# Softmax rows of the first layer turned by block transposes and an exchange through HBM, in a two-layer attention and recurrence kernel

## The chip, the cores and the metric

The kernel runs on one core of a Trainium2 chip. The time is device microseconds of one execution. The core has a matrix engine (TensorE, PE in the profile), a vector engine (VectorE, DVE), an activation engine (ScalarE, ACT), a general engine (GpSimd, POOL) and SyncE (SP), which here only issues DMA transfers. Everything is float32. A float32 matmul stands in the profile as two records, a transpose as one.

## The reference

32 batches, each an x of 128x512 and a context of 128x512, go through two layers.

```python
def layer0(x_c, x_s):                       # (128 channels, 512 positions)
    Mn = Wn @ inorm(x_c) + bn;  Mm = Wm @ inorm(x_s) + bm
    A  = softmax(Mn.T @ Mm, axis=-1)        # 512 x 512, rows t, columns s
    Ml = Wl @ x_s + bl
    Mo = Ml @ A.T                           # sum over s of Ml[c, s] A[t, s]
    return Wo @ Mo + bo + x_c
```

The second layer reads the result as 128 time steps of 512 features. It has a layer norm, a shift by one step, five mixed inputs with low-rank corrections, projections to r, k, v, g and a decay w, a recurrence over time in 32 heads of 16 (state = k v + w state; out = r (u k v + state)), a norm per head, an output projection added to the input, and a feed-forward part with squared relu and a sigmoid gate.

What matters here is the product with A.T. The scores come with t on partitions and s along the free axis, and softmax is taken along the free axis. The product sums over s, so TensorE wants A with s on partitions: the softmax rows must be turned.

## The kernel before

The 32 batches go in 8 groups of 4. `layer0(b)` (line 806) does one batch of the first layer. `layer1(g, xs)` (line 1135) does the second layer for a group, its four batches side by side as 512 columns; the batches of the next group are called inside it through `ahead`, so that both layers' instructions can be mixed.

Nothing is issued in the order in which it is written. Every call on `K` is only recorded as an operation with a cost (`cost`, line 291) and its dependences; `schedule` (line 325) then lays the operations out on the five engines by list scheduling. An operation's rank is its index, lowered by the length of the chain behind it and moved by `SHIFTS` (line 63): a number for each stage, and with a "+" one more for the last groups. A stage is a part of the work: "first0" to "first3" are the four layer-0 batches of a group, "front", "mixes", "gates", "recurrence", "values", "levels", "outputs", "head", "norm", "squares" and "rows" are parts of layer 1. The order that results is written out by hand to the engines' queues. `pace` (line 375) then looks at the loads: a load of over 500 ns is put behind a matmul of the plan, away from stretches where PE has very many small instructions. SP carries out its queue in order, so a paced load holds what stands behind it on SP until that matmul is done.

Tensors live in pools of slots that the planner hands out: 8 PSUM banks, 44 work tiles of 128x512 (`t`), 40 small ones of 128x64 (`small`), 2 `rk`, 3 `wide` of 128x1024, 4 rings of a 512x512 weight (`wring`).

In `layer0`, for each block tb of 128 positions t, one matmul gives the scores (128x512) in a bank; DVE takes the row maximum and corrects it; ACT takes the exponent into a work tile and sums it into `den`; DVE takes the reciprocal and scales the tile (line 863). The four tiles are kept in `e`. Then (lines 866 to 876), for each block sb of 128 positions s, PE transposes four 128x128 blocks into one bank, ACT copies the bank to a work tile `at`, and PE multiplies `vals` (Ml folded with Wo, s on partitions) with it, adding up over sb into the bank `po`. DVE adds the bias and x.

The constants of the first layer are loaded and folded at the start (lines 650 to 689) in tiles of their own: `WnT`, `WmT`, `Wl0`, `WoT0`, `nat0`, `nat1`, `bn_bc`.

All instructions recorded through `K` carry line 246 in the profile.

Of the kernel before, what the change touches and what calls it, by code (L numbers as in the profile page):

```python
# [12 lines left out]
F32 = mybir.dt.float32  # L13
AF = mybir.ActivationFunctionType
ALU = mybir.AluOpType
# [3 lines left out]
P = 128  # L19
# [3 lines left out]
S = 16  # L23
G = 4
NG = B // G
N = G * L
NC = E // P
# [2 lines left out]
DM, NMIX, DD = 32, 5, 64  # L30
C = 64
LEVELS = (4, 8, 16, 32)
T_SLOTS, SMALL_SLOTS, W_SLOTS, WIDE_SLOTS = 44, 40, 4, 3
Q4 = 4
EPS = 1e-5


# [23 lines left out]
SWITCH = 95  # L61
ROUNDS, TRACE, BLAME = 16, 20000, 0.001
SHIFTS = {
    "first0": -289, "first0+": -139, "first1+": -80, "first2": -32, "first2+": 88,
    "first3": -12, "first3+": 216, "front": 28, "front+": 197, "gates": -508, "gates+": 16,
    "head": -270, "head+": 164, "levels0": -88, "levels0+": -263, "levels2": -188,
    "levels2+": -623, "mixes": 64, "mixes+": -66, "norm": 56, "norm+": -145,
    "outputs0": -369, "outputs0+": -26, "outputs2": -287, "outputs2+": -673,
    "recurrence0": -21, "recurrence0+": -92, "recurrence2": 12, "recurrence2+": -88,
    "rows": 76, "rows+": 170, "squares": -98, "squares+": 56, "values0": -35,  # L70
    "values0+": -187, "values2": 33, "values2+": 116,
}
REACH, PULL = 200, 0.003
WORDS, REFILL = 280, 3200
# [19 lines left out]
class View:  # L94
# [5 lines left out]
    def at(self, slot):  # L100
        ap = self.tensor.on(slot)
        for name, args, kw in self.chain:
            if name == "view":
                offset, dims = args
                ap = bass.AP(ap.tensor, ap.offset + offset, [list(ap.ap[0]), *[list(d) for d in dims]])
            else:
                ap = getattr(ap, name)(*args, **kw)
        return ap
# [15 lines left out]

    def to_broadcast(self, shape):
        return self._then("to_broadcast", shape)

    def view(self, offset, *dims):
        return self._then("view", offset, dims)
# [245 lines left out]
def pace(order):  # L375


    tensor = [op for op in order if op.engine == "PE"]
    ends = [op.end for op in tensor]
    dense = [(op.start, op.end) for op in tensor if op.words >= 64]  # L380
    begins = [s for s, _ in dense]

    def clear(a, b):
        i = bisect.bisect_left(begins, b) - 1
        return i < 0 or dense[i][1] <= a

    behind, at = {}, 0.0
    for op in order:
        if op.calls[0][1] != "dma_start" or op.landing < 500 or not op.after:
            continue  # L390
        latest = min(a.start for a in op.after) - op.landing - 5000
        i = bisect.bisect_left(ends, max(op.start, at))
        while i < len(ends) and ends[i] <= latest and not clear(ends[i], ends[i] + 2500 + 2 * op.landing):
            i += 1
        if i < len(ends) and ends[i] <= latest:
            op.behind = tensor[i]
            behind.setdefault(tensor[i], []).append(op)
            at = ends[i] + op.landing
    paced, met = [], set()
    for op in order:  # L400
        met.add(op)
        if op.behind is None or op.behind in met:
            paced.append(op)
        paced += [x for x in behind.get(op, []) if x in met]
    return paced
# [203 lines left out]
def xattn_then_rwkv(ctx: ExitStack, tc: tile.TileContext, a: dict, out: bass.AP):  # L609
    nc = tc.nc  # L610

    const = ctx.enter_context(tc.tile_pool(name="const", bufs=1))
    psum = ctx.enter_context(tc.tile_pool(name="psum", bufs=1, space=PSUM))

    def slots(tag, count, shape, space=const):
        return [space.tile(shape, F32, tag=f"{tag}{i}", name=f"{tag}{i}") for i in range(count)]
# [1 line left out]
    banks = Pool(slots("bank", 8, [P, 512], psum))  # L618
    work = Pool(slots("t", T_SLOTS, [P, 512]))
    small = Pool(slots("small", SMALL_SLOTS, [P, 64]))  # L620
    rks = Pool(slots("rk", 2, [P, 4 * N]))
    wides = Pool(slots("wide", WIDE_SLOTS, [P, 2 * N]))
    weights = Pool(slots("wring", W_SLOTS, [P, NC * E]))
    ats = [Pool(slots(f"at{q}_", 1, [P, 2 * G * 2 * C])) for q in range(Q4)]
    vps = Pool(slots("vp", 1, [P, 2 * G * Q4 * 2 * DM]))
    for t in [t for p in ats for t in p.tiles] + vps.tiles:
        nc.vector.memset(t, 0.0)  # L627

    K = Program(nc, tc)
# [7 lines left out]
    def wide(shape=(P, 2 * N)):  # L637
        return View(Tensor(wides, list(shape)))

    def st_(*shape):  # L640
        return View(Tensor(small, [P, *shape]))


    ident = const.tile([P, P], F32, tag="ident", name="ident")
# [3 lines left out]
    eps = const.tile([P, 1], F32, tag="eps", name="eps")  # L648
    nc.gpsimd.memset(eps, EPS)
    w0 = {}  # L650
    for n in ("WnT", "WmT", "Wl0", "WoT0"):
        w0[n] = const.tile([P, P], F32, tag=n, name=n)
        nc.scalar.dma_start(w0[n], a[n])
    bias4 = const.tile([P, len(BIASES)], F32, tag="bias4", name="bias4")
    nc.scalar.dma_start(bias4, a["bias4"])
# [3 lines left out]

    nat = {}  # L660
    for i, n in enumerate(("WnT", "WmT")):
        nat[n] = const.tile([P, P], F32, tag=f"nat{i}", name=f"nat{i}")
        pn = banks.tiles[4 + i]
        nc.tensor.transpose(pn[:, 0:P], w0[n], ident)
        nc.vector.tensor_copy(nat[n], pn[:, 0:P])
# [2 lines left out]
    nc.tensor.matmul(pq[:, 0:P], nat["WnT"], nat["WmT"], start=True, stop=True)  # L668
    nc.vector.tensor_copy(wq, pq[:, 0:P])
    qwc = const.tile([P, 3], F32, tag="qwc", name="qwc")  # L670
    bn_bc = const.tile([P, P], F32, tag="bn_bc", name="bn_bc")
    nc.vector.tensor_copy(bn_bc, bias["bn"].to_broadcast([P, P]))
    pw = banks.tiles[2]
    for i, (left, right) in enumerate(
# [131 lines left out]
    def layer0(b):  # L806
        K.stage = ("first", b, str(b % G))
        x_c, x_s = wt(), wt()
        K.held = begun.get(b - 2)
        K.sync.dma_start(x_c, a["x"][b])  # L810
        K.held = begun.get(b - 2)
        K.sync.dma_start(x_s, a["ctx_2048"][b])
        stats = st_(2, 6)
        K.vector.bn_stats(stats[:, 0, :], x_c)
        K.vector.bn_stats(stats[:, 1, :], x_s)
        mv, rstd = mean_rstd(stats, 2)
        xn = []
        for i, src in enumerate((x_c, x_s)):
            xn.append(wt())
            K.vector.tensor_scalar(  # L820
                xn[i], src, mv[:, i, 0:1], rstd[:, i : i + 1], ALU.subtract, ALU.mult
            )
        x_n, y_n = xn
        pm = bank()
        K.tensor.matmul(pm, wq, x_n, start=True, stop=True)
        q = wt()
        K.scalar.activation(q, pm, AF.Identity, bias=qb)

        pc = bank()
        with K.bunch(480):  # L830
            for tb in range(NC):
                K.tensor.matmul(
                    pc[:, tb : tb + 1], x_n[:, tb * P : (tb + 1) * P], wb, start=True, stop=True
                )
        same = st_(NC)
        K.vector.tensor_scalar(same, pc[:, 0:NC], cb, None, ALU.add)


        pv = bank()
        for sb in range(NC):  # L840
            K.tensor.matmul(
                pv[:, sb * P : (sb + 1) * P], x_s[:, sb * P : (sb + 1) * P], wol,
                start=True, stop=True,
            )
        vals = wt()
        K.scalar.copy(vals, pv)


        e = []
        for tb in range(NC):  # L850
            sc = bank()
            if tb == 0:
                begun[b] = K.ops[-1]
            K.tensor.matmul(sc, q[:, tb * P : (tb + 1) * P], y_n, start=True, stop=True)
            nmax, den = st_(1), st_(1)
            K.vector.tensor_reduce(nmax, sc, AX.X, ALU.max, negate=True)

            part = same[:, tb : tb + 1]
            K.vector.scalar_tensor_tensor(nmax, nmax, part, part, ALU.subtract, ALU.add)
            t = wt()  # L860
            K.scalar.activation(t, sc, AF.Exp, bias=nmax, accum_out=den)
            K.vector.reciprocal(den, den)
            K.vector.tensor_scalar(t, t, den, None, ALU.mult)
            e.append(t)
        po = bank()
        for sb in range(NC):
            pt = bank()
            for tb in range(NC):
                K.tensor.transpose(
                    pt[:, tb * P : (tb + 1) * P], e[tb][:, sb * P : (sb + 1) * P], ident  # L870
                )
            at = wt()
            K.scalar.copy(at, pt)
            K.tensor.matmul(
                po, vals[:, sb * P : (sb + 1) * P], at, start=(sb == 0), stop=(sb == NC - 1)
            )
        K.vector.scalar_tensor_tensor(x_c, po, bol, x_c, ALU.add, ALU.add)
        return x_c


    def norm_shift(xs, w, bname, row, g):
        xns = []
# [53 lines left out]
    def recurrence(c, ex, xk, xr, xv, wk, wr, s0m):  # L936
# [13 lines left out]

        VP = G * Q4 * 2 * DM
        vp = View(Tensor(vps, [P, 2 * VP]))
        at = [View(Tensor(p, [P, 2 * G * 2, C])) for p in ats]
        for i in range(2):
            pt = bank()
            for b in range(G):
                K.tensor.transpose(pt[:, b * P : (b + 1) * P], v[i][:, b * P : (b + 1) * P], ident)
            K.scalar.copy(
                vp.view(i * VP, (2 * DM, G * Q4), (DM + S, 2), (1, S)),
                pt.rearrange("p (x y j) -> p x y j", x=G * Q4, y=2),  # L960
            )
# [56 lines left out]
        for l in LEVELS:  # L1018
# [4 lines left out]
            for x in range(2):  # L1023
# [4 lines left out]
                )  # L1028
            pa = [bank() for _ in range(Q4)]
            with K.bunch(1522):  # L1030
# [396 lines left out]
```

## Time and profile before

| what | value |
|---|---|
| runs | 1791.61, 1793.8, 1794.59 us; median 1793.8 |
| span of the profiled execution | 1791.5 us, 45991 instructions |
| granted TensorE clock, mean | 0.996 |
| DMA traffic | 87.27 MB, 14.5% of the 16 DMA engines' time on the SP queue |
| full 128x128 transposes on PE | 896 with 128 columns, 512 of them in layer 0 |

The profile counts busy time for each engine over the span, from the first to the last instruction. "128*128" behind a matmul is the part of the array that it uses, then the size of what goes through. A duration of a matmul is the time until its result is out; matmuls overlap, so the step from one start to the next is shorter. In a group of instructions the numbers behind the bar are busy time in us, mean ns of one, and the engine's idle time ahead of them with what ended it. In a table of windows, a number in brackets counts instructions, PEclk is the granted clock as a share of full speed, and the last two columns are the DMA engines' share and GB/s.

### The profile page before, as it was taken

How to read it: one execution, taken by the hardware profiler on the slowest of the kernel's cores; microseconds unless marked ns; L12 is line 12 of the kernel's file. 1: busy time of each engine (PE TensorE's matmuls, PEld its weight loads, DVE VectorE, ACT ScalarE, POOL GpSimd, SP SyncE). 2: the span in 40 equal slices, each digit the busy share in tenths (PEclk: the TensorE clock that was granted, in tenths of full speed). 3: DMA queues.
4: the chain of work that ended last, by engine and by line, in shares of the span. 5: the costliest groups of instructions: out<-in, count | busy, mean ns of one | idle time of the engine just before them, and what ended most of it. 6: DMA issues, size and time to landing. Idle time of an engine off the chain costs nothing.

```text
span 1791.5 us, 45991 instructions
## 1 busy us (share of the span) xinstructions
PE 1759.7 (98%) x20434; PEld 903.8 (50%) x20434; DVE 1195.1 (67%) x2466; ACT 681.9 (38%) x1198; POOL 313.4 (17%) x329
## 2 busy tenths in 40 slices
PE   7999999999999999999999999999999999899998
PEld 5535653456434564346543465435654445435543
DVE  8958884469835697357963679636884765866661
ACT  3424531355322553234522445224442334324321
POOL 2240015100051000500006000150010420320011
PEclk9999999999999999999999999999999999899999
DMA  6100131022020221102111021110211201000110
GB/s 192 36 0 3 43 113 66 6 64 79 30 71 1 70 74 49 52 2 88 61 48 47 2 87 61 53 41 2 88 61 59 74 25 49 3 24 3 50 36 35
DMA packets 61943, 87.27 MB, mean 49 GB/s; under 512 B 20336, under 2 KB 21488, under 8 KB 61744
## 3 DMA queue, kind: packets, MB, share of 16 engines
q1 hardware_dynamic: 61024, 84.06, 14.5%
q8 instruction: 160, 2.62, 0.6%
q14 instruction: 39, 0.32, 0.1%
q10 hardware_dynamic: 720, 0.26, 0.1%
HBM read 75.93 MB, written 8.39 MB: 47 GB/s over the span
## 4 chain that ended last, share of the span: by engine, by line
PE 89%; ACT 3%; DVE 3%; issue 3%; POOL 2%; DMA 0%; POOLq 0%; SPq 0%; ACTq 0%; DVEq 0%
PE bank L246 89%; POOL t L246 1%; DVE t L246 1%; ACT at L246 1%; DVE small L246 1%; ACT wide L246 1%; ACT t L246 0%; DMA t<-in_x_dram 0%; ACT L246 0%; DVE rk L246 0%; DVE at L627 0%; DVE vp L627 0%; POOLq L1423 0%; POOL small L246 0%; PE bank L677 0%
## 5 line engine op out<-in xcount | busy, mean ns | idle before, releaser
L246 PE MATMUL bank<-t,wring 128*128 128x512 f32 x1024 | 467.9, 599 | 0.8 <-POOL t L246 0.6
L246 PE MATMUL bank<-wring,t 128*128 128x512 f32 x768 | 340.4, 596 | 0.7 <-DVE t L246 0.7
L246 POOL TENSOR_TENSOR t<-t,t 128x512 f32<-128x512 f32 x192 | 239.2, 1282 | 426.9 <-DVE t L246 426.4
L246 PEld LDWEIGHTS bank<-t,wring 128*128 128x128 f32 x1024 | 187.2, 190 | 237.6 <-issue 211.9
L246 DVE TENSOR_TENSOR t<-bank,t 128x512 f32<-128x512 f32 (+1 forms) x256 | 143.8, 584 | 195.7 <-PE bank L246 114.8
L246 PE MATMUL bank<-t,t 128*128 128x512 f32 x512 | 255.8, 609 | 0.7 <-ACT t L246 0.2
L246 POOL TENSOR_TENSOR small<-small,neg_half 128x1 f32<-128x1 f32 (+1 forms) x96 | 65.4, 689 | 1046.0 <-DVE small L246 1046.0
L246 PEld LDWEIGHTS bank<-wring,t 128*128 128x128 f32 x768 | 143.3, 190 | 188.5 <-issue 177.6
L246 ACT COPY t<-bank 128x512 f32<-128x512 f32 (+1 forms) x240 | 132.7, 587 | 275.4 <-PE bank L246 250.3
L246 ACT ACTIVATE t<-bank 128x512 f32<-128x512 f32 x120 | 71.6, 597 | 376.4 <-PE bank L246 338.1
L246 DVE SCALAR_TENSOR_TENSOR t<-bank,vec,t 128x512 f32<-128x512 f32 x192 | 133.1, 743 | 99.3 <-PE bank L246 82.0
L246 PEld LDWEIGHTS bank<-ident,t 128*128 128x128 f32 x900 | 105.2, 141 | 71.0 <-issue 50.7
L246 ACT ACTIVATE wide<-rk,par 128x512 f32<-128x512 f32 x128 | 85.3, 714 | 131.7 <-DVE rk L246 130.9
L246 PE MATMUL bank<-ident,t 128*128 128x128 f32 x900 | 132.5, 277 | 0.3
L246 PEld LDWEIGHTS bank<-wide,rk 32*64 32x64 f32 x8192 | 95.5, 132 | 54.5 <-ACT wide L246 18.2
L246 PE MATMUL bank<-t,wv 128*128 128x512 f32 x256 | 122.6, 601 | 0.0
L246 PEld LDWEIGHTS bank<-t,t 128*128 128x128 f32 x512 | 86.0, 192 | 68.9 <-issue 40.3
L246 DVE COPY_PREDICATED at<-level,bank 128x512 f32<-128x512 int32 x192 | 120.1, 702 | 0.0
L246 PE MATMUL bank<-wide,rk 32*64 32x64 f32 x8192 | 105.5, 234 | 7.3 <-ACT wide L246 5.8
L246 ACT ACTIVATE t<-bank,small 128x512 f32<-128x512 f32 x128 | 87.5, 689 | 64.4 <-DVE small L246 63.8
L246 DVE TENSOR_REDUCE small<-bank 128x1 f32<-128x512 f32 x128 | 86.2, 683 | 24.0 <-PE bank L246 23.3
L246 DVE SCALAR_TENSOR_TENSOR t<-t,vec,t 128x512 f32<-128x512 f32 x128 | 92.0, 756 | 0.6
(114 smaller groups left out, 1828.1 us busy)
## 6 DMA issues: line engine op xcount, KB each, us to landing
t<-in_ctx_dram SPq DMA_DIRECT2D x32, 256.0 KB, 3.3
t<-in_x_dram SPq DMA_DIRECT2D x32, 256.0 KB, 3.7
wring<-in_WgT_dram SPq DMA_DIRECT2D x8, 1024.0 KB, 5.0
wring<-in_WkT_dram SPq DMA_DIRECT2D x8, 1024.0 KB, 5.1
wring<-in_WrT_dram SPq DMA_DIRECT2D x8, 1024.0 KB, 6.2
wring<-in_WoT_dram SPq DMA_DIRECT2D x8, 1024.0 KB, 5.2
out_dram<-t SPq DMA_DIRECT2D x32, 256.0 KB, 2.0
wring<-in_WfkT_dram SPq DMA_DIRECT2D x7, 1024.0 KB, 6.6
```

Source lines behind the costliest of these rows:

```text
L246: done[op] = f(*[real(x) for x in args], **{k: real(x) for k, x in kw.items()})
```

## The change

For the batches 4 to 31 (`blocks = b >= G`) the softmax rows are turned in another way; batches 0 to 3 keep the old one.

- The scaling by the reciprocal of `den` goes from DVE to ACT.
- DVE transposes each 128x512 tile in blocks of 32x32 (`vector.transpose`), reading with a stride of four elements and writing into half of a wide tile `turned`, 128x1024, that two tiles tb share. Within a block the turn is then done; which block lies on which group of 32 partitions is not.
- `exchange` puts that right: one DMA on SP's queue stores `turned` (512 KB) into a slot in HBM, a second one loads it back into another wide tile, with the 32-partition blocks in their places. Each batch has two such exchanges, one for each half of t.
- The product with `vals` runs over halves: for each half of t four matmuls of 256 columns, eight in all, in place of four of 512.
- The 16 PE transposes, the four banks for them and the four ACT copies of the batch go.
- A pool `turns` of six 512 KB slots in HBM is new. `pace` skips a DMA whose source is a tile of the planner, so the exchange's transfers aren't put behind a matmul.
- Pool sizes: work 44 to 42, wide 3 to 6, `small` 40 to 6 with 28 new `tiny` tiles of 128x16 beside it. The seven first-layer constants used only at the start lie in wide tiles now.
- `SHIFTS` has new numbers, among them "first1", "first1+", "first2+", "constants" and "front+".

```diff
-T_SLOTS, SMALL_SLOTS, W_SLOTS, WIDE_SLOTS = 44, 40, 4, 3
+T_SLOTS, SMALL_SLOTS, TINY_SLOTS, W_SLOTS, WIDE_SLOTS, RK_SLOTS, TURN_SLOTS = 42, 6, 28, 4, 6, 2, 6
 Q4 = 4
+QR = P // Q4
...
-    "first0": -289, "first0+": -139, "first1+": -80, "first2": -32, "first2+": 88,
-    "first3": -12, "first3+": 216, "front": 28, "front+": 197, "gates": -508, "gates+": 16,
...
+    "constants": -196, "constants+": 29, "first0": -289, "first0+": 238, "first1": 5,
+    "first1+": -319, "first2": -112, "first2+": 127, "first3": -12, "first3+": 210, "front": 23,
+    "front+": 310, "gates": -497, "gates+": 215, "head": -270, "head+": 201, "levels0": -58,
...
         if op.calls[0][1] != "dma_start" or op.landing < 500 or not op.after:
+            continue
+        if isinstance(op.calls[0][2][1], View):
             continue
...
+    dram = ctx.enter_context(tc.tile_pool(name="dram", bufs=1, space=bass.MemoryType.DRAM))
+    turns = Pool(slots("turn", TURN_SLOTS, [P, 2 * N], dram))
...
-        w0[n] = const.tile([P, P], F32, tag=n, name=n)
+        w0[n] = wides.tiles[i // 2][:, i % 2 * P : (i % 2 + 1) * P]
...
         e = []
+        blocks = b >= G
...
             K.vector.reciprocal(den, den)
-            K.vector.tensor_scalar(t, t, den, None, ALU.mult)
-            e.append(t)
+            if not blocks:
+                K.vector.tensor_scalar(t, t, den, None, ALU.mult)
+                e.append(t)
+                continue
+            K.scalar.activation(t, t, AF.Identity, scale=den)
+            if tb % 2 == 0:
+                turned = wide()
+            K.vector.transpose(
+                turned.view(tb % 2 * P, (QR, NC), (2 * P, Q4), (1, QR)),
+                t.view(0, (P, NC), (1, Q4), (Q4, QR)),
+            )
+            if tb % 2:
+                e.append(exchange(turned))
         po = bank()
-        for sb in range(NC):
+        for h in range(2 if blocks else 0):
+            for sb in range(NC):
+                K.tensor.matmul(
+                    po[:, h * 2 * P : (h + 1) * 2 * P], vals[:, sb * P : (sb + 1) * P],
+                    e[h].view(sb * QR, (P, 2), (2 * P, Q4), (1, QR)),
+                    start=(sb == 0 and h == 0), stop=(sb == NC - 1), skip_group_check=True,
+                )
+        for sb in range(0 if blocks else NC):
             pt = bank()
...
+    def exchange(of):
+        between, to = View(Tensor(turns, [P, 2 * N])), wide()
+        K.sync.dma_start(between, of)
+        K.sync.dma_start(
+            to.rearrange("p (i f) -> p i f", i=Q4),
+            between.whole(0, (2 * P, P), (QR * 2 * N, Q4), (1, 2 * P)),
+        )
+        return to
```

## The prediction

> **What bounds the kernel now.** I read the shares of busy time first, then the chain of waits.
>
> ```profile
> PE 1759.7 (98%) x20434; PEld 903.8 (50%) x20434; DVE 1195.1 (67%) x2466; ACT 681.9 (38%) x1198; POOL 313.4 (17%) x329
> ...
> PE 89%; ACT 3%; DVE 3%; issue 3%; POOL 2%; DMA 0%; POOLq 0%; SPq 0%; ACTq 0%; DVEq 0%
> ```
>
> TensorE (PE) is busy for 98% of the 1791.5 us span and holds 89% of the chain that ended last. The time is the length of PE's instruction stream plus a few holes, so an edit is worth what it takes out of that stream, less what it makes PE wait. The groups of instructions kept apart by shape show what the change replaces.
>
> ```profile
> L246 PE MATMUL bank<-ident,t 128*128 128x128 f32 x896 | 132.0, 277 | 0.3
> ...
> L246 ACT COPY t<-bank 128x512 f32<-128x512 f32 x208 | 115.9, 589 | 275.3 <-PE bank L246 250.3 <-issue 24.8
> ...
> L246 DVE TENSOR_SCALAR t<-t,small 128x512 f32<-128x512 f32 x128 | 61.1, 488 | 0.3
> ```
>
> The first row is all full 128x128 transposes: 16 per batch in layer 0 (512 over 32 batches) and 384 elsewhere. Their 277 ns is a latency; what one costs PE is the step from start to start, which the timeline gives.
>
> ```profile
> 396.55 1.47 PE L246 MATMUL bank<-ident,t 128*128 128x128 f32 x12
> ...
> 417.31 1.05 PE L246 MATMUL bank<-wol,t 128*128 128x128 f32 x8
> ...
> 452.95 13.90 PE L246 MATMUL bank<-wring,t 128*128 128x512 f32 x32
> ```
>
> Twelve transposes last 1.47 us: (1.47 - 0.277) / 11 = 0.108 us a step. In the same way a matmul record of 128 columns takes (1.05 - 0.275) / 7 = 0.111 us and one of 512 columns (13.90 - 0.592) / 31 = 0.429 us; a float32 matmul is two records. Last, the stretch that holds the layer-0 batches of one group, one group being some 218 us of the steady part:
>
> ```profile
> core 0: us, PE busy (x) PEld busy (x) DVE busy (x) ACT busy (x) POOL busy (x), PEclk, DMA share, GB/s
> 388.00:474.00 86.00, 85.71 (x1259) 50.64 (x1258) 74.54 (x182) 42.97 (x86) 7.98 (x11) 1.00 0.28 88
> ...
> 480.00:500.00 20.00, 19.99 (x57) 9.46 (x56) 11.30 (x22) 6.91 (x11) 0.03 (x1) 1.00 0.15 53
> 500.00:520.00 20.00, 20.00 (x61) 7.92 (x59) 7.70 (x11) 2.60 (x4) 12.02 (x10) 1.00 0.07 26
> ```
>
> There PE is full and VectorE (DVE) busy for 74.5 of 86 us; just behind it DVE is under 60% busy. DVE is the engine that the change loads.
>
> **The change part by part.**
>
> **Transposes off PE.** Batches 4 to 31, 28 of them, drop 16 transposes each: 28 x 16 x 0.109 = 48.8 us out of the stream. The row's busy time would give 132.0 / 896 = 0.147 each and 66 us, but that counts the drain under the next instruction; 48.8 is taken, 66 is the other end.
>
> **Matmuls in halves.** Four products of 512 columns become eight of 256. A 256-column record lies between the rows above: 0.111 + (0.429 - 0.111) / 3 = 0.217 us. Sixteen of them are 3.47 us, eight of 512 were 3.43: 28 x 0.04 = +1.1 us. That the weight load hides even behind 128 columns (0.111 us a step) excludes more.
>
> **ScalarE (ACT).** Per batch four PSUM copies of 589 ns go and four scalings by den come. The nearest rows are its 128x512 square out of SBUF (620 ns) and its scaling by a column (714 ns), so 112 instructions cost 3 to 14 us more. ACT is busy for 43 of 86 us in the stretch, so this is hidden and counts nothing; without that cover it would be 14 us.
>
> **DVE.** Per batch four scalings of 488 ns go and four 32x32 block transposes of 128x512 come, read with a stride of four elements. No row shows one. From below: the 488 ns scaling, nothing added. From above: the 128x1024 product, 1222 ns, +82 us of DVE in all. I take the rows nearest in shape, one pass over 128x512 at an element a step (row maximum 683 ns, product 686): 0.69 us, so 112 x (0.69 - 0.488) = +22.6 us of DVE, 0.8 us a batch, 3.2 us a group. In the stretch shown DVE would need 74.5 + 3.2 = 77.7 us, while PE would need 85.7 - 4 x 1.74 = 78.7: the two meet, and an engine that also waits on its neighbours is never wholly full. What doesn't fit must move to the stretch behind, where DVE has 8 to 12 us free in each 20. I put half of the added DVE work on the path: +11.3 us, with 0 and 22.6 as its bounds at this price, and 41 (half) at the upper price.
>
> A rule speaks against this part. The Trainium skill, page VectorE: DVE Perf Modes, section The three transpose paths (and Rules for kernel authors), says that VectorE turns 32x32 blocks only, gives 311 ns for a 128x128 in bf16 against 390 ns on TensorE, and advises TensorE for a full 128x128 whose result may go to PSUM. Four times 311 ns would be 1244 ns an instruction (an estimate for float32 from that page), +85 us of DVE, half of it on the path: 1793.8 - 48.8 + 1.1 + 42 = 1788. The trace shows 109 ns a step for TensorE's transposes and no DVE one, so the run must decide.
>
> **The exchange.** Per batch two round trips through HBM, each a 512 KB store and a 512 KB load behind it. The rows:
>
> ```profile
> t<-in_x_dram SPq DMA_DIRECT2D x32, 256.0 KB, 3.7
> ...
> wring<-in_WgT_dram SPq DMA_DIRECT2D x8, 1024.0 KB, 5.0
> ...
> out_dram<-t SPq DMA_DIRECT2D x32, 256.0 KB, 2.0
> ...
> SPq L246 <- PE bank L246: 1352.5, 77, 110.3
> ```
>
> 256 KB more cost (5.0 - 3.7) / 3 = 0.43 us, so the store lands after 2.4 us and the load after 4.1: 6.5 us a trip where the way over PE and ACT took 4 x 0.109 + 0.589, about 1 us. Nothing is held up while PE has other work queued: the second layer's projections (0.429 us a record, 32 of them in the row at 452.95) cover it, and the batch's result is only wanted by the next group. Its price is taken as 0 and its cover is PE's order; uncovered it is 28 x 5.5 = 154 us. On SP's queue 112 issues come (some 0.35 us each), and each load waits there for its own store, 56 x 2.4 = 134 us in which the x, context and weight loads and the output stores behind it stand still. SP spends 1352.5 us waiting for PE events that pace the loads, so it has room; the loads, 4 to 5 us long, are wanted only later. What is late first is an output store, which frees a work tile (ACT already waited 38.2 us in 5 places for those, and there are two tiles fewer): 0 taken, 5 waits x 2.4 = 12 us as the other end. The planner's spacing of loads away from dense PE code is skipped for these transfers; the largest "issue" wait of PE's matmuls is now 0.6 us, so if half of 112 transfers cost that, 34 us; nothing is the other end, and nothing taken, since the loads of today show under 4 us of it in total.
>
> **Slots, setup, shifts.** The constants that move into wide tiles are used before 13 us, where PE waits for the first loads anyway: 0. Pool sizes only change names of buffers: 0. The shifts set the order anew. What they can win is the holes left: around 1525 to 1575 us PE waits three times for ACT and DVE (3.05, 2.74, 1.45 us) and its clock is granted at 0.58 in the slice 1530 to 1540. Taken 0, bounds -12 (PE idle there) and +12 (a like hole elsewhere).
>
> **Sum.** Against the profiled execution: 1791.5 - 48.8 + 1.1 + 11.3 = 1755.1 us of span. The median of the runs, 1793.8, lies 2.3 above the span, so 1757 us.
>
> **The rivals.**
>
> **A. DVE becomes the bound.** If the layer-0 batches stay where they are, the stretch ends with DVE: 77.7 us of work at 93% (between the 87% of now and the 96% of its fullest 40 us, 19.55 and 18.75 of 20 each from 400 to 440) is 83.5 us. Against PE's 85.7 that is a gain of 2.2 a group in place of 7, and seven groups give 15 us: 1778. For it: DVE already at 87% there, and no work is taken off it. Against it: DVE's idle stretches next door, and the chain of waits holds only 3% DVE.
>
> **B. Slower: the exchange comes late.** PE runs in order; when the planner places the product before the load has landed, everything behind waits. The place is the 256-column product at the end of each batch, the price 5.5 us where nothing covers it. The gain of 48.8 us is used up at 1.7 us per batch, so from about a third of the trip uncovered on it decides; with 3 us uncovered, 28 x 3 = 84 us and 1793.8 - 48 + 84 = 1830. A wait of 3 us also costs clock: after the 3.05 us hole at 1529 the granted clock was 0.58 over ten us. For it: a planned 6 to 7 us trip that shares one queue with 1 MB loads. Against it: at 2 batches of slack or more the product can be placed late at no cost, and PE's own waits on a load are 6.1 us now, all at the start.
>
> **C. Contention.** The transfers cost PE its code or its tiles: the 34 or 12 us above, 1769 to 1791.
>
> **How the numbers follow.** Forecast 0.56 (1740 to 1772 by its own bounds: nothing of DVE on the path and holes closed below, all of it and some contention above), A 0.17, B 0.13, C 0.10; 0.04 for a net of nothing. A measurement of this kernel can tell about 0.2% (3.6 us) from no change. Faster takes the forecast, A and C: 0.83; same 0.04, slower B. The range 1738 to 1788 leaves out B and the ends of A, C and the shifts.
>
> **What would show it.** PE transposes fall from 900 to 452; PE's busy time falls by 45 to 66 us while its share stays near 97%; a DVE transpose at 0.69 us (over 1 us speaks for A); ACT copies fall by 112; exchange stores land in 2 to 3 us and loads in about 4. For A, DVE over 93% through the layer-0 stretch with PE idle on DVE; for B, PE waiting on DMA for the wide tiles by more than 1.7 us a batch; for C, "issue" waits over 10 us. The forecast is wrong if PE's busy time doesn't fall by about 49 us, or if holes of over 30 us open.

## The result, and the profile after

The change makes the kernel slower. Its median is 1866.7 us (1863.53 to 1874.91, four runs) against 1793.97 us for the kernel before in the same session: a ratio of 1.0417, 95% interval 1.0392 to 1.0442. The forecast was 1757 us, range 1738 to 1788. The profiled execution spans 1867.4 us; the one before spanned 1791.5.

The page of the changed kernel, first its shares of busy time, then its chain of waits by engine and by line:

```profile
PE 1757.3 (94%) x20210; PEld 923.9 (49%) x20210; DVE 1254.0 (67%) x2466; ACT 697.8 (37%) x1198; POOL 307.7 (16%) x329
...
PE 78%; DVE 9%; DMA 7%; ACT 3%; issue 2%; POOL 1%; SPq 0%; POOLq 0%; ACTq 0%; DVEq 0%
PE bank L253 78%; DMA turn<-wide 5%; DVE t L253 3%; DMA wide<-turn 3%; DVE tiny L253 2%; DVE wide L253 2%; ACT t L253 1%; ACT at L253 1%; DVE at L253 1%; DVE rk L253 0%; POOL tiny L253 0%; SPq L253 0%; DVE at L639 0%; POOL t L253 0%; DVE vp L639 0%
```

PE is busy for as long as before (1759.7 then), though by the forecast's terms it has some 48 us less to do, and its share is down from 98% to 94%. DMA, which had 0% of the chain, now has 7%, and nearly all of it is the two transfers of the exchange. The groups by shape show the new and the remaining instructions:

```profile
L253 PE MATMUL bank<-wide,t 128*128 128x256 f32 x448 | 135.7, 441 | 50.3 <-DMA wide<-turn 47.5 <-DVE t L253 2.4 <-ACT t L253 0.5
...
L253 DVE STREAM_TRANSPOSE wide<-t 128x512 f32<-128x512 f32 x112 | 123.0, 1105 | 11.4 <-ACT t L253 10.4
...
L253 PE MATMUL bank<-ident,t 128*128 128x128 f32 x448 | 68.9, 280 | 4.5 <-DVE t L253 4.4
```

The transposes on PE are down to 448, as they should be. A block transpose costs VectorE 1105 ns. The new products of 256 columns wait 47.5 us for exchange loads, in 17 places, as the first line of PE's waits says (us in total, times, longest):

```profile
PE bank L253 <- DMA wide<-turn: 47.5, 17, 5.4
```

What the DMA issues take to land (KB each, median us), from the page of the changed kernel:

```profile
turn<-wide SPq DMA_DIRECT2D x56, 512.0 KB, 2.9
wide<-turn SPq DMA_DIRECT2D x56, 512.0 KB, 4.3
```

The median transfer is as fast as expected. The view of the cores, with span and mean granted clock:

```profile
core 0: 1867.4 us, clock 0.973
```

The clock is not what it was (0.996).

Three parts account for most of the difference of 75.9 us between the two spans. PE's idle time rises from 1791.5 - 1759.7 = 31.8 to 1867.4 - 1757.3 = 110.1 us: +78. The clock's records hold full and half speed alone, so a mean clock of 0.973 means 2 x 0.027 x 1867 = 101 us at half clock, 14 us before. PE is busy in 88 of these 101 us, and in 9 of the 14; this work takes twice as long as at full clock, which costs (88 - 9) / 2 = 39 us. The third part is the forecast's own saving, -48.8 + 1.1. The sum is +70.

Where PE waits repeats from group to group. This is SP's timeline in the second group, then PE's in the same stretch:

```profile
459.61 0.38 SPq L253 DMA_DIRECT2D wring<-in_WoT_dram  x1
460.08 0.46 SPq L253 DMA_DIRECT2D turn<-wide  x1
466.84 0.37 SPq L253 DMA_DIRECT2D wide<-turn  x1
467.26 0.50 SPq L253 DMA_DIRECT2D wring<-in_WfkT_dram  x1
467.85 0.46 SPq L253 DMA_DIRECT2D turn<-wide  x1
471.89 0.37 SPq L253 DMA_DIRECT2D wring<-in_WfrT_dram  x1
475.54 0.36 SPq L253 DMA_DIRECT2D wide<-turn  x1
```

```profile
464.03 1.98 PE L253 MATMUL bank<-t,t 128*128 128x512 f32 x4
470.64 3.78 PE L253 MATMUL bank<-wide,t 128*128 128x256 f32 x8 [4.62 <-DMA wide<-turn]
...
480.51 3.78 PE L253 MATMUL bank<-wide,t 128*128 128x256 f32 x8 [1.96 <-DMA wide<-turn]
```

A 1 MB weight load is issued 0.47 us ahead of a store of the exchange. The load behind that store goes out only once the store has landed, so the distance from 460.08 to 466.84 is the store: 6.7 us instead of 2.9. The next store follows another weight load and takes from 467.85 to 475.54, 7.7 us. The products behind them start 0.05 us after the exchange has landed.

The weight load makes a store late in a second way, by its place in the queue. VectorE had finished the turn for the store of 460.08 at 457.02:

```profile
455.90 1.12 DVE L253 STREAM_TRANSPOSE wide<-t 128x512 f32<-128x512 f32 x1 [0.31 <-ACT t L253]
```

SP was waiting until 459.6 for the matmul behind which `pace` had put the weight load, and the store stood behind it: 3.06 us lost before the transfer began. Ten of the 56 stores, two for each of five groups of batches, go out 2.2 to 4.7 us after their turn is done and then take 6.7 to 9.2 us. Of the other 46 one takes 7.5 us, right behind a weight load too, and none of the rest over 4.6. The windows of this stretch give the second half of the bill:

```profile
core 0: us, PE busy (x) PEld busy (x) DVE busy (x) ACT busy (x) POOL busy (x), PEclk, DMA share, GB/s
455.00:470.00 15.00, 10.40 (x178) 6.73 (x177) 14.51 (x35) 8.57 (x14) 1.92 (x3) 0.97 0.59 179
470.00:485.00 15.00, 12.24 (x31) 7.13 (x32) 8.22 (x16) 1.39 (x3) 0.00 (x0) 0.61 0.84 278
```

After the hole of 4.62 us the clock is granted at 0.61, and the eight records of 256 columns at 470.64 take 3.78 us; twelve of them took 2.86 us at 459.46.

### The profile page after: what moved, and what is told of

Read it like the earlier page. It is cut to its first block, busy times and chain, and to the rows that moved or that the text cites. A ratio compares the mean times of both kernels' runs of the same rounds, so it can differ in the third digit from the quotient of the medians.

```text
span 1867.4 us, 45680 instructions
## 1 busy us (share of the span) xinstructions
PE 1757.3 (94%) x20210; PEld 923.9 (49%) x20210; DVE 1254.0 (67%) x2466; ACT 697.8 (37%) x1198; POOL 307.7 (16%) x329
## 4 chain that ended last, share of the span: by engine, by line
PE 78%; DVE 9%; DMA 7%; ACT 3%; issue 2%; POOL 1%; SPq 0%; POOLq 0%; ACTq 0%; DVEq 0%
PE bank L253 78%; DMA turn<-wide 5%; DVE t L253 3%; DMA wide<-turn 3%; DVE tiny L253 2%; DVE wide L253 2%; ACT t L253 1%; ACT at L253 1%; DVE at L253 1%; DVE rk L253 0%; POOL tiny L253 0%; SPq L253 0%; DVE at L639 0%; POOL t L253 0%; DVE vp L639 0%
## 5 line engine op out<-in xcount | busy, mean ns | idle before, releaser
L253 POOL TENSOR_TENSOR tiny<-tiny,neg_half 128x1 f32<-128x1 f32 (+1 forms) x96 | 59.7, 630 | 1035.7 <-DVE tiny L253 1034.5
L253 PE MATMUL bank<-wide,t 128*128 128x256 f32 x448 | 135.7, 441 | 50.3 <-DMA wide<-turn 47.5
L253 PE MATMUL bank<-t,t 128*128 128x512 f32 x288 | 148.8, 624 | 0.1
L253 PEld LDWEIGHTS bank<-wide,t 128*128 128x128 f32 x448 | 93.1, 218 | 96.4 <-DMA wide<-turn 50.3
L253 ACT ACTIVATE t<-t,tiny 128x512 f32<-128x512 f32 x112 | 79.9, 720 | 145.7 <-DVE tiny L253 145.7
L253 DVE STREAM_TRANSPOSE wide<-t 128x512 f32<-128x512 f32 x112 | 123.0, 1105 | 11.4 <-ACT t L253 10.4
L253 PE MATMUL bank<-t,wv 128*128 128x512 f32 x256 | 126.9, 607 | 1.0 <-issue 1.0
L253 DVE TENSOR_REDUCE tiny<-bank 128x1 f32<-128x512 f32 x128 | 86.6, 680 | 54.0 <-PE bank L253 53.6
L253 ACT ACTIVATE t<-bank,tiny 128x512 f32<-128x512 f32 x128 | 87.3, 683 | 88.0 <-DVE tiny L253 87.6
L253 ACT COPY t<-bank 128x512 f32<-128x512 f32 (+1 forms) x128 | 71.8, 581 | 92.0 <-PE bank L253 91.2
```

Source lines behind the costliest of these rows:

```text
L253: done[op] = f(*[real(x) for x in args], **{k: real(x) for k, x in kw.items()})
```

## The experiments

Most of the runs keep the changed kernel's order on PE, VectorE and ScalarE: the planner lays out the same plan, and one thing is altered in what is issued or in what `pace` does with the loads. Where the plan is new, this is said. The interval behind a time is that of its ratio to the kernel before.

**Loads kept clear of the exchanges.** `pace` gets the planned exchanges as stretches to avoid.

```diff
+    trips = [
+        (op.start - 3000, op.end) for op in order
+        if op.calls[0][1] == "dma_start" and op.after and isinstance(op.calls[0][2][1], View)
+    ]
     def clear(a, b):
+        if any(s < b and a < e for s, e in trips):
+            return False
```

> Same order on TensorE, VectorE and ScalarE as the changed kernel; only the paced loads (weights, x, context) keep clear of the planned exchanges, from 3 us ahead of a store to the end of its load. Theory 1 (the paced 1 MB weight loads run into the exchanges and make them late): stores land in about 3 us instead of up to 9.2, TensorE's wait for the exchange loads falls from 47.5 us to under 20, the half-clock stretches go with it, and the time falls from 1867 by 40 to 70 us, to 1800 to 1825. Theory 2 (the block transposes of 1.1 us make VectorE late, and everything behind it): the waits stay, the time stays within 15 us of 1867.

Measured: 1821.95 us, ratio 1.0163 (1.0133 to 1.0192), 45 us less than the changed kernel. PE's waits:

```profile
PE bank L253 <- issue: 18.8, 17, 3.1
PE bank L253 <- ACT t L253: 11.7, 8, 2.2
PE bank L253 <- DVE t L253: 11.7, 11, 3.0
...
PE bank L253 <- DMA wide<-turn: 4.3, 4, 1.6
```

The wait for the exchange falls from 47.5 to 4.3 us. The mean clock rises from 0.973 to 0.978 only, 80 us at half clock against 101, so the half clock goes with those waits in part. In the same place of the second group no weight load stands ahead of the stores, and they land in 3.2 and 2.6 us:

```profile
449.37 0.33 SPq L253 DMA_DIRECT2D turn<-wide  x1
452.59 0.37 SPq L253 DMA_DIRECT2D wide<-turn  x1
457.02 0.32 SPq L253 DMA_DIRECT2D turn<-wide  x1
459.69 0.37 SPq L253 DMA_DIRECT2D wide<-turn  x1
```

So theory 1 holds: what makes the exchange late is the weight loads. How much of it is their transfer and how much their place in the queue isn't separated, since the run takes both away. They come there by `pace`. In the plan of the changed kernel the four weight loads for the head of group 1 stand at 345 to 360 us of the planner's own time, and the exchanges of batches 10 and 11 at 401 to 424. `pace`, which doesn't know of exchanges, puts those loads behind matmuls at 412 to 424, in the middle of them.

**The product unhooked.** The moving tile is read from the constant `wv`.

```diff
-                    e[h].view(sb * QR, (P, 2), (2 * P, Q4), (1, QR)),
+                    apart(e[h].view(sb * QR, (P, 2), (2 * P, Q4), (1, QR))),
```

> The planned order stays and every transfer still runs, but the product of layer 0 takes its moving tile from the constant wv instead of the exchanged tile, so nothing waits for an exchange (the softmax rows are left out of the result). Theory 1 and theory 3 (a round trip is too long for the plan whether or not a load is in the way): the wait of 47.5 us and most of the half clock go, 1867 falls to 1770 to 1800. Theory 2 (VectorE): the plan waits for VectorE instead, the time stays above 1830.

Measured: 1816.71 us, ratio 1.0134 (1.0089 to 1.0178). Taking the wait away altogether gives 50 us, only 5 more than moving the loads. That is above the range stated, so the wait for the exchange is the larger part of the loss and not all of it.

**No exchange.** As above, and the 112 transfers are not issued.

```diff
+            if op.calls[0][1] == "dma_start" and op.after and isinstance(op.calls[0][2][1], View):
+                continue
```

> As the run with the unhooked product, and the two transfers of each exchange are left out too (the softmax rows are left out of the result). What the transfers cost others by their traffic and their place in the queue is the difference from that run: under theory 1 and 2 less than 10 us; if the traffic itself slows code fetch, loads or stores, 15 us or more.

Measured: 1807.36 us, ratio 1.0081 (1.0052 to 1.0111), 9.4 us less than with the transfers running. That lies just under the 10 us stated for "little", and with two executions of each the two intervals overlap, so the size is uncertain. Where it may go can be read. PE's waits on "issue", in which it waits for nothing that the profile shows, with the transfers and without:

```profile
PE bank L254 <- issue: 17.4, 16, 2.5
PE bank L256 <- issue: 6.2, 12, 2.6
```

The increase is ahead of the short, dense products, above all `bank<-at,vp` (12.4 us against 2.4). That code fetch is delayed there is a possible reading; no run isolates it.

**A copy for the turn.**

```diff
-            K.vector.transpose(
+            K.vector.tensor_copy(
                 turned.view(tb % 2 * P, (QR, NC), (2 * P, Q4), (1, QR)),
```

> Same order on every engine; the 32x32 block transposes are replaced by a plain VectorE copy with the same access patterns (the turn within the blocks is left out of the result), the exchange stays. The copy should take 0.5 to 0.7 us instead of 1.105, 45 to 65 us less of VectorE. Theory 2: the exchanges start 1 us or more earlier, and the time falls by 40 us or more, to under 1827. Theory 1: the stores still meet the weight loads and the time stays above 1840.

Measured: 1865.65 us, ratio 1.0407 (1.0371 to 1.0442), with the copy at 732 ns. VectorE is 34 us lighter and nothing moves: behind a late exchange it doesn't matter when the turn ends.

**A copy for the turn, without the exchange.** The two edits together.

> As the run without the exchange, and a plain VectorE copy (0.732 us in the run with the copy) stands for the block transpose (1.102 us): 41 us less VectorE work on the same planned order; the softmax rows are left out of the result. Theory 2b (with the exchange out of the way, the block transposes are what remains: holes of 1.5 to 3 us where TensorE waits for VectorE and ACT, each followed by half clock): 1807 falls by 15 us or more, to under 1792. Theory 4 (the holes are in the new plan itself, whatever a turn costs): within 8 us of 1807.

Measured: 1784.77 us, ratio 0.9966 (0.9954 to 0.9978), as theory 2b said. Against 1807.36 the same 112 x (1.102 - 0.743) = 40 us of VectorE now bring 22.6 us, or 20.6 by the two ratios (the kernel before ran 3 us faster beside this run). So the price of the turn does lie on the path, to 51 to 56%, once the exchange doesn't cover it. This run has neither a turn nor an exchange and is still 28 us over the forecast of 1757.

**Turns reading neighbours.** The turn takes 32 neighbouring elements instead of every fourth.

```diff
-                t.view(0, (P, NC), (1, Q4), (Q4, QR)),
+                t.view(0, (P, NC), (QR, Q4), (1, QR)),
```

> The changed kernel, its block transposes reading 32 neighbouring elements instead of every fourth (the positions s come out in another order, so the result's softmax rows are permuted). If the stride of four makes the transpose dear, its mean falls from 1.105 to 0.6 to 0.75 us; if the turn itself does, it stays at 1.05 to 1.11. The time stays within 8 us of 1867 either way, since the run with the copy showed that a cheaper VectorE instruction alone moves nothing.

Measured once: 1859.84 us. VectorE's group of turns:

```profile
L253 DVE STREAM_TRANSPOSE wide<-t 128x512 f32<-128x512 f32 x112 | 78.1, 702 | 12.5 <-ACT t L253 11.5
```

Reading with a stride of four elements costs the turn 0.40 us of its 1.105; reading neighbours it takes 0.70. The stride alone doesn't make an instruction that dear: the copy with the same patterns took 0.732. The time hardly moves, as in the run with the copy.

**The old turn with the new slots and shifts.** A new plan.

```diff
-        blocks = b >= G
+        blocks = False
```

> All of the change's pool sizes and shifts, but all 32 batches turned on TensorE as before; the plan is made anew. If the shifts and slots alone cost nothing, 1780 to 1805; if they are what leaves holes (theory 4), 1810 or more with granted clock under 0.99.

Measured: 1849.45 us, ratio 1.033 (1.03 to 1.036). The shifts and slots of the change together, put under the old turn, cost 59 us; the run doesn't separate them.

**The new turn with the old shifts.** A new plan; the `SHIFTS` of the kernel before in the changed kernel.

> The change with the shifts of the kernel before, planned anew, nothing else touched: weight loads still meet the exchanges. If the new shifts are worth their place for the new turn, it is slower than 1867 by 10 us or more; if the shifts are what harms, it comes under 1850.

Measured: 1935.3 us, ratio 1.0788 (1.0767 to 1.081). So the new shifts are worth 69 us to the new turn. Each set of shifts fits one program, and neither can be priced alone.

**The planner told the true price.** Loads clear, the turn at 1.1 us in `cost`, a new plan.

```diff
             "bn_aggr": 100,
+            "transpose": 75 + 2.0 * n,
```

> Loads clear of the exchanges as in the first run of that name, and the planner told 1.1 us for a block transpose instead of 0.6, so the order is planned anew with the change's shifts. If the holes left at 1822 come from the planner's wrong price (theory 2b), the granted clock rises over 0.985 and the time falls to 1780 to 1808; if from the shifts and the thinner TensorE filler, it stays at 1810 to 1835.

Measured: 1859.04 us, ratio 1.0383 (1.0342 to 1.0425), outside both ranges that were stated. With the shifts of the change, which were fitted to the wrong price, the plan made with the true price is worse than the plan with the wrong price and clear loads by 37 us. It has more holes (DVE ends 24.9 us of PE's waits, against 11.7).

**A repaired version.** Loads clear, and the stride moved from the four turns of a batch to the one instruction that normalizes the context; the order of s is then right for a turn of neighbours. The plan is that of the changed kernel.

```diff
             xn.append(wt())
+            turned_in = xn[i].view(0, (P, NC), (QR, Q4), (1, QR)) if i and b >= G else xn[i]
             K.vector.tensor_scalar(
-                xn[i], src, mv[:, i, 0:1], rstd[:, i : i + 1], ALU.subtract, ALU.mult
+                turned_in, src.view(0, (P, NC), (1, Q4), (Q4, QR)) if i and b >= G else src,
+                mv[:, i, 0:1], rstd[:, i : i + 1], ALU.subtract, ALU.mult
             )
...
-                t.view(0, (P, NC), (1, Q4), (Q4, QR)),
+                t.view(0, (P, NC), (QR, Q4), (1, QR)),
```

> A repaired version of the change, same planned order: loads clear of the exchanges, and the stride of four moved from the four block transposes of a batch to the one VectorE instruction that makes the normalized context (its result is written in the order that the turn wants), so the transposes read 32 neighbours. Transposes 0.70 us instead of 1.105 (45 us less VectorE), that one instruction 0.55 to 0.95 us. If the two causes found so far add up (45 us from the loads, 22 us from the turn's price, the difference of the two runs without an exchange), 1867 - 45 - 22 = 1800, 1790 to 1808; if the turn's price is hidden once the exchanges are back, 1815 to 1825.

Measured: 1802.64 us, ratio 1.0047 (1.003 to 1.0064). The two repairs add up: 45 us from the loads, 19 us from the turn. The page's busy line, then PE's longest waits:

```profile
PE 1730.4 (96%) x20210; PEld 913.2 (51%) x20210; DVE 1220.2 (68%) x2466; ACT 697.7 (39%) x1198; POOL 309.0 (17%) x329
```

```profile
PE bank L253 <- issue: 23.0, 24, 2.6
PE bank L253 <- ACT t L253: 9.8, 8, 2.1
PE bank L253 <- DVE t L253: 7.5, 5, 3.0
```

PE's busy time is 29 us under that of the kernel before, its idle time 1801.3 - 1730.4 = 71 us against 32, and the clock 0.987. The waits on "issue" are now the largest; the kernel before had 3.1 us of them.

**The shifts set anew.** The repaired version with the turn at 0.70 us in `cost` and new shifts, found by a search in the planner alone; once from the shifts of the kernel before, once from those of the change.

> The repaired version (loads clear of the exchanges, turns on neighbouring elements), the planner told 0.70 us for a turn, and the shifts set anew for that, starting from those of the kernel before; holes of TensorE over 1.2 us in the plan were counted 1.7 us extra. If the 8 us by which the repaired version is behind the kernel before lie in holes of the old plan and the half clock after them, half-clock time falls from 49 to under 35 us and the time to 1770 to 1792; if they lie in what the exchange traffic does to code fetch (23 us of issue waits), it stays at 1795 to 1810.

> As the run before it, the shifts set anew starting from those of the change; its plan has more holes. The same two outcomes: 1775 to 1797 if holes decide, 1795 to 1812 if the code fetch does.

Measured: 1826.35 us, ratio 1.0201 (1.0164 to 1.0239), and 1812.34 us, ratio 1.0116 (1.0095 to 1.0136). Both miss what was stated, the second by 0.3 us. PE's idle time did not fall on the chip: 80 and 72 us against 71 in the repaired version (clock 0.981 in both, issue waits 27.0 and 18.5 us). The planner's own ends beside the measured times (us) show how little the one says of the other here:

```
version                      planner's end   measured
before                       1739.4          1793.5
the change                   1719.4          1866.7
loads clear                  1719.4          1822.0
repaired                     1719.4          1802.6
old turn, new shifts         1769.2          1849.5
true price, shifts of change 1775.3          1859.0
set anew from the change     1736.4          1812.3
set anew from before         1730.5          1826.4
```

The planner counts on the change being 20 us faster. In the change it prices a turn at 0.60 us, doesn't know of the clock, and plans loads that `pace` then moves. No version with the exchange beat the kernel before.

## Why the prediction was wrong, by its own steps

**What bounds the kernel.** Right, and it is why everything below counts: PE's stream was full, and each wait put into it showed in the time.

**Transposes off PE, matmuls in halves.** Right. 448 transposes are gone, and twelve records of 256 columns in (2.86 - 0.441) / 11 = 0.220 us a step stand against the 0.217 that was interpolated. Counted with its half-clock time by half, PE's busy time falls from 1755 to 1713.5 us: 42 of the 47.7 us are there. They are hidden under 78 us of new idle time and 39 us of slow clock, so the prediction's own signs of being wrong came: PE's busy time did not fall, and holes of over 30 us opened.

**ACT.** The scaling takes 720 ns, at the dear end of the two rows named; ACT's busy time rises by 16 us, 2 over the upper bound. It isn't what decides.

**The turn on VectorE.** The term was mis-sized: 1.105 us where 0.69 was taken, so VectorE got 59 us (1195.1 to 1254.0) instead of 22.6. The bounds, 0.488 and 1.222, held it. The row maximum and the product read neighbouring elements, and read that way the turn does take 0.70; what they don't price is the turn with a stride, and the strided copy, at 0.732, wouldn't have priced it either. The share on the path, put at one half without a row that showed it, came out: 51 to 56% without the exchange, and 19 of some 38 us in the repaired version. In the change itself it didn't show, because the late exchange covered it. The rule weighed there, from the Trainium skill's page VectorE: DVE Perf Modes, section The three transpose paths, made four times 311 ns, 1244 ns; the chip took 1105 with the stride and 702 without, so the estimate from the page was nearer to what was built than the row taken was, and too high for the turn alone.

**The exchange.** This is the step that failed: "Its price is taken as 0 and its cover is PE's order", and, on SP's queue, "it has room; the loads, 4 to 5 us long, are wanted only later". The trip itself was sized well: with nothing else on the queue a store lands in 2.7 us (median) and its load mostly in 3.6 to 3.9, against 2.4 and 4.1. But room on average is not room in the right place. That loads are wanted only later is exactly what lets `pace` move them, and it moved them onto the exchanges, where a store goes out up to 4.7 us late and then takes 6.7 to 9.2 us. The prediction named the skip in `pace` and asked only what the exchange does to PE's code, not what the paced loads do to the exchange. Where the prediction put 0, the price was 45 us by moving the loads, 50 by removing the wait.

**Rival B** was this mechanism, with the same place (the product at a batch's end). It expected 3 us uncovered at each of 28 batches; on the chip 17 places have 47.5 us, 1.7 us a batch. With the other waits PE's idle time rose by 78 us, near the 84 of its sum; the 39 us of slow clock, for which it has no term, are what its 1830 lacks.

**The clock.** Named in a sentence under B and given no term. All of PE's holes together cost half as much again in clock, 39 us for 78 us more of idle time, because holes of 1 to 5 us are spread over every group. Here a page and the runs differ: the Trainium skill, page TensorE: Matmul & The Clock Gate, section Part 1: The HAM clock gate, puts the drop behind an idle window of some 3.4 us. In the run without the exchange half clock follows a hole of 1.46 us. Its PE timeline shows the hole, and two windows the clock behind it (columns as in the windows above):

```profile
904.20 1.14 PE L256 MATMUL bank<-t,heads_t 8*128 8x512 f32 x8 [1.46 <-DVE tiny L256]
```

```profile
902.00:906.00 4.00, 2.49 (x12) 0.75 (x11) 4.00 (x6) 1.39 (x3) 0.00 (x0) 1.00 0.65 249
906.00:910.00 4.00, 4.00 (x10) 2.74 (x9) 4.00 (x7) 0.00 (x0) 0.00 (x0) 0.57 0.82 261
```

PE is idle for 1.46 us ahead of 904.20, the clock is full until 906 and granted at 0.57 behind it. The measurement decides: no idle window of 3.4 us was needed. But the length of a hole alone doesn't decide either. In the kernel before, a longer one, 1.69 us, left the clock at 1.00 until 1531:

```profile
1402.12 1.12 PE L246 MATMUL bank<-t,w 128*128 128x512 f32 x2 [1.69 <-DVE t L246]
```

What else decides stays open.

**Slots and shifts**, "Taken 0, bounds -12 (PE idle there) and +12 (a like hole elsewhere)", was wrong in kind: the change's shifts and slots move the old turn by +59 us, and its shifts, against the old ones, move the new turn by -69.

**Rivals A and C.** VectorE did become dear (21 to 23 us of the path in the runs without an exchange), and in those windows it is busy for all of 8 us from 902 to 910. The sign named for A, a transpose of over 1 us, came, but A is not what slowed the change: PE's waits on VectorE's tiles `t` are 14.9 us there, those on the exchange 47.5, and a cheaper instruction in the turn's place moved nothing. Of C, its sign came too ("issue" waits over 10 us: 14.5 in the change), and the run without the transfers is 9.4 us faster at the medians; that they delay code isn't shown.

**What stays open.** The copy without an exchange is 28 us over the forecast. Its idle time (1784.8 - 1733.3 = 52 us) and its clock (0.985) are large enough for it: 20 us more idle time than before and (50 - 9) / 2 = 20 us of slow clock, by PE's busy time at half clock, where the forecast allowed some 11 us for VectorE on the path. What leaves those holes, and whether another plan could close them, wasn't shown; the two sets of shifts tried didn't.

## What to carry to other kernels

When an engine at 98% is relieved by moving work to transfers, look at what else stands in the same queue at that moment, and above all at anything that moves loads late on purpose: those loads will meet the new transfers. Price a hole in TensorE's stream twice, once for the wait and once for the slow clock that may follow it. Price a VectorE instruction by a row of the same operation with the same element stride; where there is none, a row of the same size, or another operation with the same stride (the copy, 0.732 us for a turn of 1.105), is only a bound.

## What the runs showed of the hardware that was not expected

- A block transpose of 128x512 float32 on VectorE takes 0.702 us when it reads neighbouring elements and 1.105 us when it reads every fourth; a plain copy with the strided patterns took 0.732.
- In the changed kernel a 512 KB store to HBM lands in 2.6 to 4.2 us (median 2.7, 29 stores) with nothing else on its queue, and in 6.7 to 9.2 us (11 stores) when a 1 MB load was issued up to 0.8 us ahead of it on the same queue.
- With traffic that no product waits for, PE's waits on "issue" were 17.4 us against 6.2 without; the time between the two runs, 9.4 us, is not clear of their noise.
- Half clock came behind holes in TensorE's stream far shorter than 3.4 us, 1.46 us in one place, though not behind every one (1.69 us in another); in the changed kernel 110 us of idle time went with 101 us of it.
